# A second Strassen level for one more product, its operands in the large buffers, and another order of the steps

## The chip, the cores and the metric

The kernel runs on one core of a Trainium2 chip. Its engines are TensorE (PE; PEld is its weight load), VectorE (DVE), ScalarE (ACT), GpSimd (POOL) and SyncE (SP), whose queue issues nearly all transfers. The metric is device time in microseconds (us), as the median of several executions. A profile is one execution, recorded instruction by instruction.

## The reference

Eight sequences of 1024 tokens with 1024 features, all float32, get a cross attention and then a linear layer, each behind a layer norm and each added to its input:

```python
# x [8,1024,1024], memory m [8,64,1024], mask [8,64], factors [8,1024,1024], bias [1024]
x = x + attention(layernorm(x), m, mask)          # softmax(q m^T / 32) m, per sequence
x = x + einsum('btd,rde->bte', layernorm(x), factors) / sqrt(8) + bias
```

The sum over the eight factors does not depend on the token, so the kernel first adds the factors to one 1024 x 1024 matrix and then multiplies once.

## The kernel before, in words

**Groups and pairs.** The 8192 tokens are 16 groups `g` of 512: four row tiles `x[g, t]` of 128 tokens. Row tiles 0 and 2 are pair q = 0, tiles 1 and 3 pair q = 1 (`t = 2 h + q`).

**The attention of a group.** Tokens come twice: as row tiles (`load_rows`, L306) and as blocks (`load_blocks`, L295) which DVE transposes (`transpose_blocks`, L351). The first two groups are transposed by PE instead (`transpose_x_pe`, L377). `scores` (L394), `scores_back`, `softmax` (L422), `weights_back` and `read_out` (L460) are the attention; `residual` (L470, DVE) adds it to the rows. Row statistics come from DVE (`row_stats`, L336) or from ACT and POOL (`row_sums` and `row_squares`, L311 and L321).

**The second norm.** Per pair, either `norm_stats` (L480, DVE: two bn_stats of 512 columns and one aggregation for each h) or `norm_sums` and `norm_squares` (L499, L509: ACT passes and short POOL steps), then `normalize` (L525, ACT), which writes a large buffer `h`. `relayout` (L548) moves it by 16 transfers on SP's queue to `hb`, and `transpose_rows` (L557, DVE) makes `hT`. Group 0 is transposed by PE (`transpose_h_pe`).

**The big product.** Each pair has 256 rows, a 2 x 2 of blocks 128 rows x 512 features; the factor matrix is a 2 x 2 of 512 x 512 quadrants. A Strassen-Winograd scheme needs seven products instead of eight (`PRODUCTS`, L195). Row combinations s1 to s4 are `combine_rows` (L569, DVE), factor combinations t1 to t4 come out of `add_sums` (L711). `product g q p` (L587) is four matmuls of 128 x 512, each two records in the trace; `give` (L603, DVE) adds the result, scaled, from PSUM to one or two half row tiles.

**The second level.** For products 2, 3 and 4 (`SECOND`, L194) the two pairs together form a 2 x 2 again, with one operand of 256 rows, and seven smaller products take the place of two: `combine_parts` (L611, four DVE combinations of 128 x 256), `part` (L636, two matmuls of 128 x 256, four records) and `give_part` (L652, DVE, 256 columns for each of the product's outputs). The factor operands of the parts are four quadrants of the operand (one of them overwritten) and three new ones in `tau`, made once by `combine_factors` (L727).

**Factors.** The 32 `load_factor` transfers (1 MB each; s is the slice of rows, r the rank) are added up either on DVE (`add_factor`, L678) or on PE by an identity (`sum_factor`, L696, into PSUM).

**Buffers.** Large buffers of 8 KB a partition are handed out first in, first out (`Slots`, L155; `bigs`, L171): factors, `xb`, `xT`, `h`, `hb`, `hT` and the centred memory share eight. Row tiles have eleven slots, PSUM eight banks.

**Order.** Nothing reorders the work: `START` (L24) and `LOOP` (L78) are written-out lists of steps, and each engine and each DMA queue works off its own instructions in that order. `LOOP` runs 17 times; in it g is the group in its big product, p = g - 1, n = g + 1 (attention and norm), m = g + 2 (loads and scores). A step that is done already, or whose group doesn't exist, is skipped (`run`, L741).

```python
    SECOND = (2, 3, 4)
...
        5: ("s1", "t1", "v", True, ((1, 1), (0, 1)) if 3 in SECOND else ((1, 1),)),
...
    tau = const.tile([P, 3 * len(SECOND), 2 * HH], F32, name="tau")
```

Of the kernel before, what the change touches and what calls it, by code (L numbers as in the profile page):

```python
# [10 lines left out]
F32 = mybir.dt.float32  # L11
# [13 lines left out]
load_memory 0; load_factor 0 6; add_factor 0 6; centre_memory 0; load_rows 0 0; load_bias;  # L25
constants; load_factor 0 4; load_rows 0 3; load_rows 0 2; add_factor 0 4; load_rows 0 1;
load_factor 0 7; row_stats 0 0; transpose_x_pe 0 1; load_factor 1 2; row_stats 0 1;
transpose_memory 0; load_factor 0 0; transpose_x_pe 0 0; scores 0; masks; scores_back 0;
row_stats 0 2; add_factor 1 2; row_stats 0 3; add_factor 0 0; load_factor 0 5; load_factor 0 3;
load_factor 1 0; softmax 0; load_factor 1 5; sum_factor 0 5; load_factor 2 7; weights_back 0;  # L30
read_out 0 0 0; load_factor 0 2; add_factor 1 5; load_factor 2 6; add_factor 1 0; sum_factor 0 3;
read_out 0 0 1; residual 0 0 1; residual 0 0 0; load_factor 0 1; sum_factor 0 7; add_factor 0 2;
load_factor 2 4; read_out 0 1 1; norm_stats 0 0 0; sum_factor 0 1; load_rows 1 1; add_factor 2 6;
load_rows 1 0; norm_stats 0 0 1; add_factor 2 4; normalize 0 0 0; add_sums 0 1; residual 0 1 1;
normalize 0 0 1; load_factor 1 7; load_factor 2 3; load_factor 2 5; load_factor 1 4;
transpose_h_pe 0 0 0; sum_factor 2 7; add_factor 1 7; load_factor 1 3; transpose_x_pe 1 0;
load_factor 1 6; add_sums 0 0; transpose_h_pe 0 0 1; read_out 0 1 0; add_factor 2 3;
add_bias 0 0 2; add_bias 0 0 3; sum_factor 2 5; load_rows 1 3; load_factor 1 1; residual 0 1 0;
norm_stats 0 1 0; sum_factor 1 4; sum_factor 1 1; load_factor 2 1; load_rows 1 2;
combine_rows 0 0 1; sum_factor 2 1; norm_stats 0 1 1; add_factor 1 3; load_factor 2 2;  # L40
add_factor 1 6; load_factor 2 0; add_sums 1 1; row_sums 1 0; load_factor 3 0; add_sums 1 0;
transpose_x_pe 1 1; add_factor 2 2; add_factor 2 0; add_bias_v 0 0 0; add_bias_v 0 0 1;
add_sums 2 1; row_squares 1 0; load_factor 3 4; add_factor 3 4; scores 1; add_factor 3 0;
add_sums 2 0; product 0 0 1; load_factor 3 2; normalize 0 1 0; normalize 0 1 1;
transpose_h_pe 0 1 0; load_factor 3 3; add_factor 3 3; row_sums 1 1; load_factor 3 1;
load_factor 3 6; combine_rows 0 0 2; load_factor 3 7; transpose_h_pe 0 1 1; product 0 0 5;
row_squares 1 1; combine_rows 0 0 3; load_factor 3 5; add_factor 3 2; sum_factor 3 1;
combine_rows 0 0 4; scores_back 1; sum_factor 3 6; give 0 0 1; load_rows 2 1; load_rows 2 0;
add_factor 3 7; combine_rows 0 1 1; sum_factor 3 5; softmax 1; add_sums 3 1; row_sums 2 0;
product 0 1 1; weights_back 1; product 0 0 6; add_sums 3 0; read_out 1 0 0; combine_parts 0 4 1;  # L50
combine_factors 4; residual 1 0 0; read_out 1 0 1; combine_rows 0 1 2; part 0 4 2; give 0 0 6;
part 0 4 1; give_part 0 4 1; combine_parts 0 4 2; combine_rows 0 1 3; part 0 4 5; residual 1 0 1;
load_blocks 2 1; load_blocks 2 0; combine_rows 0 1 4; product 0 0 7; give 0 1 1;
norm_stats 1 0 0; row_squares 2 0; give_part 0 4 2; combine_parts 0 4 3; read_out 1 1 0;
add_bias 0 1 0; add_bias 0 1 1; norm_stats 1 0 1; product 0 1 6; part 0 4 6; combine_parts 0 2 1;
load_rows 2 2; residual 1 1 0; read_out 1 1 1; combine_parts 0 4 4; give_part 0 4 6; give 0 1 6;
residual 1 1 1; product 0 1 5; normalize 1 0 0; product 0 1 7; give_part 0 4 5;
combine_factors 3; normalize 1 0 1; load_memory 2; combine_factors 2; part 0 4 7; give 0 0 5;
give_part 0 4 7; give 0 0 7; part 0 4 3; part 0 2 1; transpose_blocks 2 0 0; part 0 2 5;
norm_sums 1 1; centre_memory 2; transpose_blocks 2 0 1; give_part 0 4 3; combine_parts 0 2 2;  # L60
give_part 0 2 1; transpose_blocks 2 0 2; part 0 4 4; combine_parts 0 3 1; transpose_memory 2;
relayout 1 0; give_part 0 4 4; part 0 3 1; part 0 3 2; add_bias 1 0 0; add_bias 1 0 1;
transpose_blocks 2 1 0; store 0 2; part 0 2 6; give_part 0 3 2; part 0 3 5;
transpose_blocks 2 1 1; give_part 0 2 5; norm_squares 1 1; transpose_blocks 2 0 3;
transpose_blocks 2 1 2; part 0 2 2; normalize 1 1 0; combine_parts 0 2 3; transpose_blocks 2 1 3;
normalize 1 1 1; give_part 0 2 6; combine_parts 0 2 4; combine_parts 0 3 2; transpose_rows 1 0 0;
scores 2; load_rows 2 3; transpose_rows 1 0 1; combine_rows 1 0 1; give_part 0 2 2; part 0 2 7;
# [40 lines left out]
def kernel(  # L108
# [632 lines left out]
    def run(line: str, groups):  # L741
        name, *args = line.split()
        args = [groups[a] if a in groups else int(a) for a in args]
        if groups:
# [3 lines left out]
            if name.endswith("memory") and g % GPB:  # L748
                return
# [38 lines left out]
```

## Time and profile before

| | us |
|---|---|
| median of 3 runs | 965.39 (964.19 to 966.02) |
| the profiled execution | 964.01 |
| its span | 962.2 |
| PE busy | 931.7 (97%) |
| DVE busy | 801.4 (83%) |
| ACT busy | 380.8 (40%) |
| POOL busy | 259.5 (27%) |
| transfers | 167.01 MB, mean 174 GB/s |

The span runs from the first to the last instruction on record; the remaining 1.8 us of the profiled execution lie around it. In a group's line of the profile the name left of the arrow is what is written, the names right of it what is read; `y4u` is a PSUM sum of parts of product 4, `yu` one of first-level products. Busy time is counted once where instructions of an engine overlap, while the mean is that of single records, so for pipelined work the distance between two starts tells more than a duration.

### The profile page before, as it was taken

The page shows a single profiled execution, that of the slowest core. Times are in us where ns is not written, and L with a number is a line of the kernel's source. Part 1 is how long each engine was busy: PE and PEld are TensorE (multiplying, and loading weights), DVE is VectorE, ACT ScalarE, POOL GpSimd, SP SyncE. Part 2 cuts the span into 40 slices and gives each one's busy share as a digit, 9 for nine tenths or more (in the row PEclk, how much of TensorE's full clock was granted, in tenths as well). Part 3 has the DMA queues.
Part 4 walks back from the last instruction along what each step waited for, and adds up shares of the span by engine and source line. Part 5 has one row for each costly group of instructions (what it writes and reads, how often), then busy time and mean ns, then how long its engine had stood idle before and what let it go on. Part 6 is the DMA issues. An engine that isn't in the chain of part 4 may idle for free.

```text
span 962.2 us, 11083 instructions
## 1 busy us (share of the span) xinstructions
PE 931.7 (97%) x3456; PEld 546.7 (57%) x3456; DVE 801.4 (83%) x1511; ACT 380.8 (40%) x712; POOL 259.5 (27%) x361
## 2 busy tenths in 40 slices
PE   3889999999999999999999999999999999999998
PEld 2345455655656565564656566564656566565656
DVE  3699999979799787988789787988789787988865
ACT  3036253443625254352724345351714445352300
POOL 0031125322322242421323142331324233232300
PEclk9999999999999999999999999999999999999999
DMA  9999736466565756457575746557575746552412
GB/s 352 419 421 397 182 101 145 127 184 156 160 163 161 162 171 153 135 159 174 157 167 159 169 140 158 141 170 175 154 180 153 174 112 181 139 158 79 101 66 87
DMA packets 93530, 167.01 MB, mean 174 GB/s; under 512 B 12320, under 2 KB 71840, under 8 KB 89376
## 3 DMA queue, kind: packets, MB, share of 16 engines
q1 hardware_dynamic: 93024, 165.20, 59.5%
q10 hardware_dynamic: 448, 1.11, 0.3%
q8 instruction: 27, 0.44, 0.2%
q14 instruction: 31, 0.25, 0.1%
HBM read 101.25 MB, written 33.55 MB: 140 GB/s over the span
## 4 chain that ended last, share of the span: by engine, by line
PE 87%; DMA 5%; DVE 5%; issue 1%; SPq 1%; ACT 0%; DVEq 0%; ACTq 0%
PE yu L594 33%; PE yv L594 11%; PE scT L401 6%; PE y3u L643 6%; PE y2u L643 6%; PE y4u L643 6%; PE ro L467 6%; DMA f<-in_L_ffn_factors_dram 4%; PE y4v L643 3%; PE y3v L643 3%; PE y2v L643 3%; PE y3z L643 1%; PE y2z L643 1%; PE y4z L643 1%; DMA x<-in_x_dram 1%; DVE b L691 1%
## 5 line engine op out<-in xcount | busy, mean ns | idle before, releaser
L543 POOL TENSOR_TENSOR x<-x,bias_bc 128x512 f32<-128x512 f32 x126 | 170.9, 1377 | 70.4 <-DVE x L607 35.8
L536 ACT ACTIVATE h<-x,nb,rstd 128x512 f32<-128x512 f32 x128 | 96.3, 825 | 211.4 <-DVE x L475 145.3
L594 PE MATMUL yu<-b,hT 128*128 128x512 f32 x256 | 118.0, 604 | 0.0
L594 PE MATMUL yu<-t,s 128*128 128x512 f32 x256 | 115.2, 593 | 0.0
L594 PE MATMUL yv<-t,s 128*128 128x512 f32 x256 | 115.2, 592 | 0.0
L594 PE MATMUL yu<-t,hT 128*128 128x512 f32 x256 | 115.1, 592 | 0.0
L607 DVE SCALAR_TENSOR_TENSOR x<-yu,x 128x512 f32<-128x512 f32 x128 | 83.2, 679 | 28.0 <-PE yu L594 28.0
L475 DVE SCALAR_TENSOR_TENSOR x<-ro,rden,x 128x512 f32<-128x512 f32 x128 | 88.5, 743 | 3.8 <-PE ro L467 3.8
L318 ACT ACTIVATE junk<-x 128x1024 bf16<-128x1024 f32 x60 | 63.3, 1055 | 49.1 <-DMA x<-in_x_dram 48.2
L594 PEld LDWEIGHTS yu<-b,hT 128*128 128x128 f32 x256 | 46.3, 189 | 62.6 <-issue 51.8
L358 DVE STREAM_TRANSPOSE xT<-xb 128x256 f32<-128x256 f32 x224 | 81.7, 411 | 0.0
L594 PEld LDWEIGHTS yu<-t,hT 128*128 128x128 f32 x256 | 48.6, 190 | 54.4 <-issue 50.2
L562 DVE STREAM_TRANSPOSE hT<-hb 128x1024 f32<-128x1024 f32 x60 | 73.6, 1228 | 3.1 <-DMA hb<-h 2.9
L594 PEld LDWEIGHTS yu<-t,s 128*128 128x128 f32 x256 | 48.5, 190 | 48.2 <-issue 45.7
L594 PEld LDWEIGHTS yv<-t,s 128*128 128x128 f32 x256 | 48.5, 190 | 48.2 <-issue 45.9
L492 POOL TENSOR_SCALAR rstd<-mv 128x2 f32<-128x2 f32 x17 | 4.6, 269 | 245.6 <-DVE mv L489 245.6
L330 ACT ACTIVATE junk<-x,nmean 128x1024 bf16<-128x1024 f32 x60 | 68.9, 1149 | 3.0 <-POOL nmean L319 0.8
L467 PE MATMUL ro<-mem,eT 64*128 64x512 f32 x256 | 64.5, 617 | 0.6 <-ACT eT L456 0.6
L657 DVE SCALAR_TENSOR_TENSOR x<-y3u,x 128x256 f32<-128x256 f32 x64 | 26.2, 410 | 44.6 <-PE y3u L643 44.4
L401 PE MATMUL scT<-xT,memT 128*64 128x256 f32 x512 | 60.5, 383 | 0.0
L504 ACT ACTIVATE junkz<-x 128x1024 bf16<-128x1024 f32 x30 | 31.7, 1056 | 67.7 <-DVE x L475 67.2
L706 PE MATMUL sum<-f,ident 128*128 128x512 f32 x96 | 43.7, 601 | 7.3 <-DMA f<-in_L_ffn_factors_dram 7.1
(133 smaller groups left out, 1495.5 us busy)
## 6 DMA issues: line engine op xcount, KB each, us to landing
f<-in_L_ffn_factors_dram SPq DMA_DIRECT2D x32, 1024.0 KB, 11.2
x<-in_x_dram SPq DMA_DIRECT2D x64, 512.0 KB, 4.5
out_dram<-x SPq DMA_DIRECT2D x64, 512.0 KB, 4.6
hb<-h SPq DMA_DIRECT2D x480, 64.0 KB, 2.0
xb<-in_x_dram SPq DMA_DIRECT2D x112, 256.0 KB, 7.0
mem<-in_ctx_dram SPq DMA_DIRECT2D x14, 256.0 KB, 3.9
mem<-in_ctx_dram ACTq DMA_DIRECT2D x2, 256.0 KB, 5.4
bias_bc<-in_L_ffn_bias_dram ACTq DMA_DIRECT2D x1, 512.0 KB, 7.8
```

The costliest lines, as they stand in the source:

```text
L318: nc.scalar.activation(junk, st["x", g, t], AF.Copy, accum_out=s1[:, t : t + 1])
L330: nc.scalar.activation(junk, st["x", g, t], AF.Square, bias=nmean[:, t : t + 1], accum_out=ss[:, t : t + 1])
L358: nc.vector.transpose(xT[:, 2 * e + c].rearrange("p (t j) -> p t j", j=Q), xb.rearrange("p t (k e i c) -> p e c t k i", e=NC // 2, i=2, c= ...
L401: nc.tensor.matmul(ps[ts(h, M), : 2 * P], mT[:, c, :], st["xT", g, h][:, c, :], start=(c == 0), stop=(c == NC - 1),)
L467: nc.tensor.matmul(ps, eT[ts(h, M), q, :], m[ts(h, M), ts(n, H)], start=True, stop=True)
L475: nc.vector.scalar_tensor_tensor(xt, st.pop(("ro", g, q, n, h)), rden[:, k : k + 1], xt, ALU.mult, ALU.add)
L536: nc.scalar.activation(to, fr, AF.Identity, bias=nb[:, h : h + 1], scale=rstd[:, h : h + 1])
L543: eng.tensor_add(xt, xt, bias_bc[:, ts(k % 2, H)])
L562: nc.vector.transpose(st["hT", g, q][:, h].rearrange("p c (t j) -> p t c j", j=Q), hb[:, h].rearrange("p t (c i) -> p t c i", i=Q),)
L594: nc.tensor.matmul(ps, lhs[:, c, :], wq[right][:, c, :], start=(first and c == 0), stop=(c == KH - 1), skip_group_check=True,)
L607: nc.vector.scalar_tensor_tensor(xt, st["y", g, q, key], ISR, xt, ALU.mult, ALU.add)
L643: nc.tensor.matmul(ps, lhs[:, c, :], wp[p][i][:, c, :], start=(first and c == 0), stop=(c == 1), skip_group_check=True,)
```

## The change

Product 5 is put among the second-level products. Its operand s1 of the two pairs is combined, and its factor operand t1 gets three more combinations. `tau` no longer has a place of its own: twelve operands, four to a buffer, lie in three large buffers that `combine_factors` takes and never gives back, and there are ten large buffers in place of eight. Parts 1, 2 and 3 read raw quadrants and may run ahead of `combine_factors`. Group 0 keeps the undivided product 5, and its steps of parts are skipped. The order is new throughout: `START` loads tokens of groups 0 and 1 ahead of the factors, and finishes more of group 1's attention early; slices s = 0, 1 and 3 of the factors come ahead of s = 2. Row statistics of group 1 move to `row_stats`, and the second norm of all groups goes by `norm_sums` and `norm_squares`; no bias addition is left on DVE.

```diff
 START = """
-load_memory 0; load_factor 0 6; add_factor 0 6; centre_memory 0; load_rows 0 0; load_bias;
-constants; load_factor 0 4; load_rows 0 3; load_rows 0 2; add_factor 0 4; load_rows 0 1;
...
+load_rows 1 0; constants; load_rows 0 0; load_rows 0 1; load_rows 0 2; load_memory 0;
+row_stats 1 0; load_rows 1 1; transpose_x_pe 0 0; row_stats 0 0; centre_memory 0; load_rows 0 3;
+transpose_x_pe 1 0; load_rows 1 2; masks; transpose_memory 0; load_factor 0 5; add_factor 0 5;
...
+sum_factor 2 7; load_factor 2 0; add_bias 0 0 3; add_factor 2 3; part 0 4 2; load_factor 2 5;
+combine_parts 0 4 2; add_factor 2 1; sum_factor 2 0; product 0 1 5; combine_rows 0 0 4;
+add_factor 2 4; give_part 0 4 2; combine_parts 0 4 3; load_memory 2; load_rows 2 0;
+normalize 1 0 1; relayout 1 0; add_factor 2 5; centre_memory 2; normalize 1 1 0; add_sums 2 1;
+product 0 0 6; load_blocks 2 1; add_sums 2 0; add_bias 0 1 3; give 0 0 6; transpose_memory 2;
+part 0 4 1; combine_factors 4; product 0 0 7; give_part 0 4 1; combine_parts 0 4 4; part 0 4 5;
...
+combine_rows 1 0 2; row_squares 2 0; combine_factors 3; relayout 1 1; scores 2; product 1 0 6;
+scores_back 2; give 0 1 7; combine_factors 5; give_part 0 2 6; part 0 3 6; part 0 2 2;
...
 LOOP = """
...
-add_bias g 1 3; combine_rows g 0 4; read_out n 1 0; norm_stats n 0 0; combine_rows g 1 2;
-read_out n 1 1; norm_stats n 0 1; transpose_blocks m 0 0; part g 4 5; end_rows p 1; end_rows p 0;
...
+load_blocks m 1; give_part p 3 7; part p 2 4; transpose_rows g 1 0; transpose_rows g 1 1;
+part p 3 4; weights_back n; combine_rows g 0 3; give_part p 3 2; give_part p 2 3; part p 3 3;
+combine_rows g 1 1; combine_rows g 0 4; load_blocks m 0; product g 1 1; give_part p 2 4;
+give_part p 3 4; give_part p 3 3; combine_parts g 5 1; read_out n 0 0; read_out n 0 1;
+part g 5 5; end_rows p 0; residual n 0 0; residual n 0 1; read_out n 1 0; residual n 1 0;
+norm_sums n 0; read_out n 1 1; combine_rows g 1 2; give g 1 1; give g 0 6; combine_parts g 5 2;
...
+transpose_rows n 0 0; normalize n 1 1; give_part g 5 4; give_part g 3 1; store g 2; scores m;
+combine_parts g 3 2; transpose_rows n 0 1; part g 3 5; product n 0 1; combine_rows n 0 1;
+combine_parts g 3 3; load_rows m 2; give_part g 2 6; give g 1 7; part g 3 6; row_sums m 1;
+scores_back m; relayout n 1; store g 3; combine_rows n 0 2; part g 2 7; add_bias g 0 1;
...
-    bigs = Slots(big, [f"big{i}" for i in range(8)])
+    bigs = Slots(big, [f"big{i}" for i in range(10)])
...
-    SECOND = (2, 3, 4)
+    SECOND = (2, 3, 4, 5)
...
-    tau = const.tile([P, 3 * len(SECOND), 2 * HH], F32, name="tau")
+    NTAU = 3 * len(SECOND)
+    tau = []
+    if NTAU % 4:
+        rest = const.tile([P, NTAU % 4, 2 * HH], F32, name="tau")
     wp = {}
-    for j, p in enumerate(SECOND):
+
+    def quadrant(p: int, i: int):
+
         w = wq[PRODUCTS[p][1]]
-        t1, t3, t4 = (tau[:, 3 * j + k, :].rearrange("p (c n) -> p c n", c=2) for k in range(3))
-        wp[p] = {1: w[:, :2, :HH], 5: t1, 6: w[:, :2, HH:], 3: w[:, 2:, HH:], 7: t3, 2: w[:, 2:, :HH], 4: t4}
+        return {1: w[:, :2, :HH], 3: w[:, 2:, HH:], 2: w[:, 2:, :HH]}[i]
...
+        right = quadrant(p, i) if i in (1, 2, 3) else wp[p][i]
...
-                wp[p][i][:, c, :],
+                right[:, c, :],
...
-        w = wp[p]
+        n = 3 * len(wp)
+        while len(tau) < n + 3:
+            k = len(tau)
+            four = rest if k >= NTAU - NTAU % 4 else bigs.take(("tau", k), [P, 4, 2 * HH], f"tau_{k}")
+            tau.extend(four[:, i, :].rearrange("p (c n) -> p c n", c=2) for i in range(four.shape[1]))
+        w = wp[p] = {i: quadrant(p, i) for i in (1, 2, 3)}
+        w.update({6: wq[PRODUCTS[p][1]][:, :2, HH:], 5: tau[n], 7: tau[n + 1], 4: tau[n + 2]})
...
+            if name in ("combine_parts", "part", "give_part") and ("product", g, 0, args[1]) in done:
+                return
```

## The prediction, made before the changed kernel was run

> **What bounds the kernel now.** I read the busy line first, then the slices, then the windows, the timeline of one period and the chain.
>
> ```profile
> PE 931.7 (97%) x3456; PEld 546.7 (57%) x3456; DVE 801.4 (83%) x1511; ACT 380.8 (40%) x712; POOL 259.5 (27%) x361
> ...
> PE   3889999999999999999999999999999999999998
> ...
> DVE  3699999979799787988789787988789787988865
> ...
> DMA  9999736466565756457575746557575746552412
> ```
>
> PE is full from the fourth slice to the last but one; DVE is close behind; the DMA engines are full for four slices, while the 32 factors stream in. So there are two regimes, and the windows give their sizes (columns: window, length, then busy time of PE, PEld, DVE, ACT, POOL, granted clock, DMA share, GB/s).
>
> ```profile
> 0.00:20.00 20.00, 3.71 (x17) 3.41 (x18) 6.26 (x11) 5.36 (x8) 0.96 (x8) 1.00 0.89 337
> 20.00:40.00 20.00, 18.94 (x90) 10.02 (x91) 12.18 (x18) 5.49 (x16) 1.23 (x2) 1.00 1.01 422
> 40.00:60.00 20.00, 15.34 (x60) 7.60 (x58) 18.35 (x24) 7.50 (x13) 3.86 (x6) 1.00 1.02 420
> 60.00:80.00 20.00, 17.40 (x62) 8.77 (x62) 17.75 (x23) 4.49 (x9) 4.41 (x5) 1.00 1.01 419
> 80.00:100.00 20.00, 19.10 (x74) 9.55 (x71) 19.90 (x23) 11.97 (x21) 3.67 (x5) 1.00 0.98 389
> ...
> 484.74:538.80 54.06, 54.06 (x201) 31.89 (x200) 45.42 (x88) 21.14 (x36) 14.79 (x22) 1.00 0.60 157
> ```
>
> Until 100 us PE works 74.5 us and idles 25.5: it waits for DMA. In a later period of 54.06 us (one loop pass, 484.74 to 538.80) it idles not at all, at full clock, and DVE works 45.4 us. After 100 us a microsecond off PE's work is a microsecond off the end, as long as nothing else comes late.
>
> **Part 1: product 5 by parts, PE.** Groups 1 to 15 lose two products (8 matmul records each) and gain seven parts (4 records each). Starts in the timeline give their real spacing; the durations overlap.
>
> ```profile
> 507.24 1.03 PE L643 MATMUL y4u<-t,r 128*128 128x256 f32 x4
> 508.10 3.60 PE L594 MATMUL yu<-t,s 128*128 128x512 f32 x8
> 511.53 1.03 PE L643 MATMUL y2v<-tau,r 128*128 128x256 f32 x4
> 512.40 1.03 PE L643 MATMUL y2u<-b,hT 128*128 128x256 f32 x4
> ```
>
> A product takes 511.53 - 508.10 = 3.43 us, a part 0.86 (nine parts run from 511.53 to 519.30: 0.863 each). 2 x 3.43 - 7 x 0.863 = 0.82 us less per group, **12.3 us** in 15 groups. The new parts have the form of the 336 measured ones, so a part that costs more is excluded.
>
> **Part 1: DVE.** Starts again:
>
> ```profile
> 479.78 0.42 DVE L657 SCALAR_TENSOR_TENSOR x<-y3u,x 128x256 f32<-128x256 f32 x1 [3.20 <-PE y3u L643]
> 480.12 0.68 DVE L607 SCALAR_TENSOR_TENSOR x<-yu,x 128x512 f32<-128x512 f32 x1
> 480.71 0.42 DVE L657 SCALAR_TENSOR_TENSOR x<-y2u,x 128x256 f32<-128x256 f32 x1
> ```
>
> A give of 512 columns costs 0.59, one of 256 costs 0.34. Product 5 feeds two outputs, so each part is given twice: 14 x 0.34 = 4.8 against 4 x 0.59 = 2.4. The four combinations of the new product cost (35.0 + 34.2 + 24.1 + 19.9) / 48 = 2.4 us by their groups. The new loop takes the statistics of both halves of the normalization on ACT, which removes two norm_stats (2 x (2 x 0.64 + 0.21) = 3.0 us). Sum: +1.8 us, DVE 47.2 of 53.2 us (89%, now 84%). ACT gains 2 x (1.06 + 0.19 + 1.15 + 0.19) = 5.2, about 29 of 53. Neither reaches PE; that slack is what hides these edits, and a DVE instruction that PE waits for costs its delay if the slack is used up.
>
> **Where a rule speaks against it.** The row:
>
> ```profile
> L629 DVE TENSOR_TENSOR hT<-hT,hT 128x256 f32<-128x256 f32 x48 | 35.0, 730 | 0.0
> ```
>
> The median of these is 418 ns, the longest 1491 ns, and the long ones (1.36 and 1.49 us at 512.60 and 513.88) lie under POOL's bias additions (512.40 to 515.08). The Trainium skill (SBUF — State Buffer, Who interferes with whom) says that a DVE instruction with two SBUF inputs is shut out while a GpSimd instruction reads SBUF, and one with a single SBUF input is not. By that only the four combinations per group can be held, not the 14 gives, which read PSUM; were each held for a whole bias addition of 1377 ns (the row of L543), DVE would stand at 47.2 + 5.5 = 52.7 us of 53.2, with no slack left. By the rows the means already hold such waits (2.4 us, not 4 x 0.34), and I take those.
>
> **Part 2: three of ten large buffers.** After the start seven serve the loop instead of eight. I followed each take to the release it reuses. Most have 5 to 18 us of PE work between. The thin one: in every other group h of the second pair takes the buffer that relayout of the first pair frees. Relayout is 16 DMAs on SP's queue:
>
> ```profile
> 504.99 10.18 SPq L553 DMA_DIRECT2D hb<-h  x16
> ```
>
> plus 2.0 us to land. The chain in a new pass, counted from its start: last residual of the second pair at 19, ACT's two row sums (2.5) and the first pair's normalize (3.0) to 24.5, relayout 12.2 to 36.7, second normalize 3.0 to 39.7, second relayout 12.2 to 51.9. Its transpose is wanted at the next pass's start plus 2.8 us less 1.2, 54.8: slack 2.9 us. So I charge nothing; queued behind a late second relayout on SP are only store g 3 and the next blocks, and its waiter is DVE, then PE. Store g 2 stands ahead of it on SP and needs its tile's last give: rival 2 has the price. The Trainium skill (Perfetto Trace Analysis, Optimization Strategy) warns that the same gap repeated on the busy engine can mean too few buffers for the next tile; before shows no such gap, and the rule has no price.
>
> **Part 3: tokens first.** Before, PE's first transpose starts at 16.29 us, behind two factors and four row tiles. The new order asks for rows ahead of all factors: two row tiles behind one other, 2.1 MB with the memory, against 4.7 MB before. At the first window's 337 GB/s those 4.7 MB are 14.0 us, 2.3 short of 16.29; so 6.2 + 2.3 = 8.5 us. That is worth only what is done before the next barrier. The chain shows it:
>
> ```profile
> 93.19 6.06 DMA f<-in_L_ffn_factors_dram
> 99.29 3.71 PE sum L706 x8
> ```
>
> The last factor lands at 99.2, and product 6 of group 0 needs t2, so all factors; it starts at 106.48. Both orders issue the same 38.8 MB up to the last factor (32 of 1.05 MB, eight row tiles, memory, bias), so it can't land much earlier than 99; ten buffers instead of eight let the loads run as far ahead. Then, new: add_factor 2.3 us, two sums 1.2, t2 1.15 gives 103.8; DVE may be behind, so I take 105, **1.5 us** earlier. Bounds: 420 GB/s throughout lands it at 95.5, product 6 at 100 (-6.5); a stalled SP queue, +4. What PE has done by then: all that it had before plus the four read_outs of group 1 (4 x 0.96), product 0 1 5 (3.43) and one part (0.86): **8.1 us** more. In all that is 42.8 for sums, 13.7 for products, 0.9, 13.6 for transposes, 15.7 for scores, weights and read-outs: 87 us of the 96 from 8.5 on. DVE worked 80.4 us of the first 106.2 before, from 12.75 on; with four more residuals (5.3) and its other new work at most 88, of the 100 from 5 on. Twelve sum_factor and 20 add_factor stay as they were, and norm_stats of group 0 and row statistics of group 1 change places between DVE and ACT: nothing.
>
> After that barrier DVE is the late one. From product 6 on, `scores 2` follows five products, eleven parts and the memory's transposes, 17.2 + 9.5 + 0.6 = 27.3 us of PE. It reads the blocks that DVE transposes, and ahead of the last of them DVE has add_sums 2.3, two combine_factors 5.2, four gives 3.0, nine part gives 3.0, twelve combinations 6.1, two transpose_rows 2.3 and eight transpose_blocks 5.5: 27.4 us by free spacings. From 106.5 to 165.2 DVE took 57.9 us for work that I count at 54.1 in the same way, 7% over: 29.3, after 1.2 for t3, 30.5. That is 3 us of waiting; with a second, smaller one where parts of product 3 need combine_factors 3, **4 us** back. Bounds 0 and 8 (twice that).
>
> **Tail.** The last pass has the same end, a few parts, then stores; one bias addition (1.38 us) is put at the end, but on POOL, which is idle, for a half tile whose last give isn't the last. Nothing, at most 1.4.
>
> **Sum.** Span 962.2 - 12.3 - 1.5 - 8.1 + 4 = 944.3; the profiled execution took 964.0 for that span, 1.8 us outside it, so **946** us. The runs' median, 965.39, is 0.14% above the profiled time, inside the 0.2% that a measurement of this kernel can tell from no change.
>
> **Rivals.**
> 1. *Waits eat part of it* (20%). DVE at 89% has no spare in the passages where it leads PE by under 1 us (combine_parts 5 1 is listed directly ahead of part 5 5, behind one product). If PE waits 0.8 us in each of 15 groups, the Strassen saving is gone and the start's remains: 958. For it: the "DVE x <- PE y" waits show that DVE runs just behind PE; against it: PE idled 0.0 us in the period above.
> 2. *Slower* (14%): the second relayout comes late behind store g 2. SP's waits at L668 for DVE's combinations are 86.3 us in 22 and 56.8 in 9, 4.6 us each. One such wait against a slack of 2.9 in 14 groups costs 24 us: 970. It makes the kernel slower than before when the 18 us of gain are used up, that is from 1.3 us of PE idle per group, a wait of 4.2 us. Against it: the tile of store g 2 gets its last give some 4 us of PE work before the store's place.
> 3. *The start goes better* (8%): DMA full throughout, no wait at `scores 2`: 946 - 5 - 4 = 937.
> That the change doesn't do what it says has no room in the steady groups; in group 0 product 5 stays undivided, which the count of 15 holds.
>
> **How the numbers follow.** Forecast 946 (58%, own range 940 to 952). The range reaches down to rival 3's 937 and up through most of rival 1, 962; out of it are rival 2 and a little. Faster by over 0.2% (under 963.5): 0.83; within: 0.03; slower: 0.14.
>
> **What would show it.** PE busy near 919 us; no L594 matmul of yv after the start (t1's product), 28 parts per group; steady period 53.2; DVE near 89%; first transpose at 8 to 9 us; product 6 of group 0 at 105; a wait of PE at scores 2. I would be wrong if PE shows the same idle in every pass (on DVE: rival 1; on hb: rival 2), or if the first 100 us still hold 25 us of idle.

## The result, and the profile after

The changed kernel takes **949.24 us** (median of 4 runs, 948.81 to 951.26) against 964.79 us for the kernel before on the same chip (964.02 to 966.02): ratio 0.9835, 95% interval 0.9823 to 0.9847. It was predicted at 946.0, range 937 to 962. The profiled execution took 949.06 us, its span is 947.2 us, so 1.9 us lie outside the span.

The page of the changed kernel, busy line and three of its slices:

```profile
PE 921.2 (97%) x3636; PEld 579.9 (61%) x3636; DVE 794.2 (84%) x1633; ACT 453.2 (48%) x832; POOL 278.3 (29%) x359
...
PE   4979999999999999999999999999999999999998
...
PEclk9979999999999999999999999999999999999999
DMA  9979876567484856658484756648484755641412
```

PE's work fell from 931.7 to 921.2 us, near the 919 that was predicted, and from the fourth slice on PE is as full as before. But the third slice has a dent in three rows at once: PE, the granted clock and DMA. In the profiled execution of before the clock was at full speed throughout and DMA stood at 9 for four slices. (The profile of before shows one execution with a mean granted clock of 1.00; 27 of its 34 executions timed beside the later runs had 0.995 or 0.996, and all four of the changed kernel 0.993 or 0.994.) The sum came out nearly right while one of its terms was badly wrong, and it is hidden there.

**The loop** does what was forecast. From the start of one group's `scores` to that of another twelve groups on, the chain of before gives (853.27 - 197.72) / 12 = 54.63 us a group:

```profile
197.72 3.60 PE scT L401 x32
...
853.27 3.60 PE scT L401 x32
```

and that of the changed kernel (837.49 - 192.88) / 12 = 53.72:

```profile
192.88 3.60 PE scT L404 x32
...
837.49 3.60 PE scT L404 x32
```

That is 0.91 less, against 0.82 predicted; in 600 us from 250 on PE idles 0.15 us.

**The start** does not. Product 6 of group 0, which needs all factors, begins at 114.43 us, where before had 106.48 and the prediction 105. The timeline of PE in before:

```profile
106.48 3.60 PE L594 MATMUL yu<-t,s 128*128 128x512 f32 x8
```

and in the changed kernel:

```profile
114.43 3.70 PE L597 MATMUL yu<-t,s 128*128 128x512 f32 x8 [1.11 <-DVE t L726]
```

From there to the end it takes 947.2 - 114.4 = 832.8 us, against 962.2 - 106.5 = 855.7 before. To see why that product is late, read the windows of the changed kernel around the dent (window, length, busy PE, PEld, DVE, ACT, POOL, granted clock, DMA share, GB/s):

```profile
44.00:48.00 4.00, 3.17 (x12) 1.08 (x11) 4.00 (x5) 0.00 (x0) 4.00 (x1) 1.00 1.02 426
...
52.00:56.00 4.00, 1.31 (x8) 0.88 (x8) 1.90 (x2) 3.97 (x7) 0.00 (x0) 0.86 1.02 426
56.00:60.00 4.00, 2.56 (x4) 0.99 (x4) 0.66 (x1) 3.97 (x8) 0.22 (x1) 0.50 1.00 418
60.00:64.00 4.00, 3.86 (x6) 1.68 (x7) 3.48 (x6) 0.07 (x1) 1.10 (x3) 0.50 0.65 270
64.00:68.00 4.00, 4.00 (x13) 1.93 (x12) 1.03 (x2) 0.00 (x0) 0.00 (x0) 0.86 0.02 6
```

In time order: POOL is busy for 4 us with one instruction while DVE is full; then PE starves; then the clock falls to half; then DMA stops, in the middle of loading the factors. The timeline of the changed kernel has the first link:

```profile
43.42 1.22 DVE L695 TENSOR_TENSOR b<-b,f 128x1024 f32<-128x1024 f32 x1
43.58 6.78 POOL L522 TENSOR_SCALAR rstd<-zq 128x2 f32<-128x2 f32 x1 [2.63 <-ACT junky L518]
...
49.09 1.23 DVE L695 TENSOR_TENSOR t<-t,f 128x1024 f32<-128x1024 f32 x1
50.22 1.41 DVE L478 SCALAR_TENSOR_TENSOR x<-ro,rden,x 128x512 f32<-128x512 f32 x2
...
51.47 3.02 ACT L539 ACTIVATE h<-x,nb,rstd 128x512 f32<-128x512 f32 x4 [7.97 <-POOL nb L525]
...
57.23 2.56 PE L470 MATMUL ro<-mem,eT 64*128 64x512 f32 x4 [3.15 <-ACT hT L377]
```

A step on two numbers per partition, 0.19 us at 60.16, takes 6.78 us. It begins just after the first of six additions of factors on DVE, each with two inputs in SBUF, and ends at 50.36, 0.14 us after DVE has come to `residual`, which reads PSUM. ACT waits 7.97 us for it, PE waits for ACT, and PE's later matmuls run at half clock (four read-outs in 2.56 us, elsewhere 1.1). The loads stop at 62 us because no large buffer comes back: SP's queue waited up to 15.9 us in one place for PE's transposes, whose input `h` would have freed one.

### The profile page after: what moved, and what is told of

Read it like the earlier page. It is cut to its first block, busy times and chain, and to the rows that moved or that the text cites. A ratio compares the mean times of both kernels' runs of the same rounds, so it can differ in the third digit from the quotient of the medians.

```text
span 947.2 us, 11708 instructions
## 1 busy us (share of the span) xinstructions
PE 921.2 (97%) x3636; PEld 579.9 (61%) x3636; DVE 794.2 (84%) x1633; ACT 453.2 (48%) x832; POOL 278.3 (29%) x359
## 4 chain that ended last, share of the span: by engine, by line
PE 90%; DVE 5%; DMA 1%; issue 1%; POOL 1%; ACT 1%; SPq 0%; DVEq 0%; ACTq 0%
PE yu L597 34%; PE ro L470 6%; PE scT L404 6%; PE y5u L647 6%; PE y2u L647 6%; PE y4u L647 6%; PE y3u L647 6%; PE y3v L647 3%; PE y5v L647 3%; PE y2v L647 3%; PE y4v L647 3%; DVE b L695 2%; PE y2z L647 1%; PE y3z L647 1%; PE y5z L647 1%; PE y4z L647 1%
## 5 line engine op out<-in xcount | busy, mean ns | idle before, releaser
L507 ACT ACTIVATE junkz<-x 128x1024 bf16<-128x1024 f32 x64 | 67.6, 1057 | 109.3 <-DVE x L478 108.3
L597 PE MATMUL yu<-b,hT 128*128 128x512 f32 x256 | 115.1, 593 | 0.1
L597 PE MATMUL yu<-t,hT 128*128 128x512 f32 x256 | 112.6, 592 | 0.0
L478 DVE SCALAR_TENSOR_TENSOR x<-ro,rden,x 128x512 f32<-128x512 f32 x128 | 88.6, 745 | 17.8 <-PE ro L470 17.7
L509 POOL TENSOR_SCALAR zm<-zs 128x2 f32<-128x2 f32 x32 | 13.2, 411 | 248.6 <-ACT junkz L507 248.6
L518 ACT ACTIVATE junky<-x,zm 128x1024 bf16<-128x1024 f32 x64 | 73.5, 1149 | 13.6 <-POOL zm L509 11.3
L597 PEld LDWEIGHTS yu<-b,hT 128*128 128x128 f32 x256 | 48.5, 190 | 49.2 <-issue 47.2
L321 ACT ACTIVATE junk<-x 128x1024 bf16<-128x1024 f32 x56 | 59.0, 1054 | 30.4 <-DMA x<-in_x_dram 29.8
L333 ACT ACTIVATE junk<-x,nmean 128x1024 bf16<-128x1024 f32 x56 | 64.3, 1149 | 7.5 <-POOL nmean L322 5.3
L404 PEld LDWEIGHTS scT<-xT,memT 128*64 128x64 f32 x512 | 35.3, 137 | 21.1 <-issue 4.3
L322 POOL TENSOR_SCALAR nmean<-sum 128x2 f32<-128x2 f32 x28 | 7.5, 267 | 136.1 <-ACT junk L321 136.1
## 6 DMA issues: line engine op xcount, KB each, us to landing
x<-in_x_dram SPq DMA_DIRECT2D x64, 512.0 KB, 3.6
out_dram<-x SPq DMA_DIRECT2D x64, 512.0 KB, 3.2
mem<-in_ctx_dram ACTq DMA_DIRECT2D x2, 256.0 KB, 10.2
bias_bc<-in_L_ffn_bias_dram ACTq DMA_DIRECT2D x1, 512.0 KB, 8.1
```

The source lines that it names most:

```text
L404: nc.tensor.matmul(ps[ts(h, M), : 2 * P], mT[:, c, :], st["xT", g, h][:, c, :], start=(c == 0), stop=(c == NC - 1),)
L478: nc.vector.scalar_tensor_tensor(xt, st.pop(("ro", g, q, n, h)), rden[:, k : k + 1], xt, ALU.mult, ALU.add)
L507: nc.scalar.activation(junk, st["x", g, 2 * h + q], AF.Copy, accum_out=s1[:, h : h + 1])
L518: nc.scalar.activation(junk, st["x", g, 2 * h + q], AF.Square, bias=nmean[:, h : h + 1], accum_out=ss[:, h : h + 1])
L597: nc.tensor.matmul(ps, lhs[:, c, :], wq[right][:, c, :], start=(first and c == 0), stop=(c == KH - 1), skip_group_check=True,)
```

## Experiments

**Theory S** (starved step): POOL's step is the root, and clock, buffers and the hole in DMA follow from it. **Rival O**: the order on ACT, which has two more passes (54.39 to 56.6) ahead of the copy of hT, is the root. **Rival M**: the last factor is late through the large buffers alone, so that none of the first three moves changes the time (949). The first four kernels were timed beside before at 965.70 us, the next four beside 965.40, three more beside 964.70, the last beside 964.04.

### 1. Two residuals between the additions

```diff
-residual 0 1 1; load_factor 1 7; residual 0 1 0; add_factor 0 6; add_factor 1 7; sum_factor 1 0;
+load_factor 1 7; add_factor 0 6; residual 0 1 0; add_factor 1 7; residual 0 1 1; sum_factor 1 0;
```

> START alone is changed: the two residuals of group 0's second pair move from ahead of three add_factor steps into the run of them (one behind add_factor 0 6, one behind add_factor 1 7). They read PSUM, so the run of DVE additions with two SBUF inputs is broken at 45.7 and 49.3 us. Theory S (a 0.2 us POOL step of group 0's norm was shut out for 6.8 us by that run; the late h idles PE, PE's clock falls, buffers come back late, DMA idles 6 us, product 6 of group 0 starts at 114.4 in place of 105): the POOL step rstd takes under 1 us, h of the first pair starts near 47 in place of 51.5, granted clock 1.00 from 50 to 70, no hole in the DMA rate at 62 to 68, product 6 at 106 to 108, time 941 to 944. Rival O (the order on ACT is the root: the row sums of the second pair stand ahead of the copies of hT): PE still waits 2 to 3 us for hT, clock still falls, time 947 to 949. Rival M (the last factor is late by the slots alone): no change, 949.

945.29 us, ratio 0.9787 (0.9765 to 0.9809); product 6 at 110.29. POOL's step took 0.92 us and ended as `residual` began:

```profile
46.30 0.92 POOL L519 TENSOR_SCALAR rstd<-zq 128x2 f32<-128x2 f32 x1 [2.63 <-ACT junky L515]
```

An earlier step of POOL, 0.32 us in the changed kernel, now stood under two additions; it took 2.59 us and ended at 43.67, 0.17 us after the residual behind them began. DMA still fell, but to 0.54 at 62 to 66, and the clock to half for 3.4 us, behind a wait of PE of 1.69 us for the moved residual. The direction is S's and M falls; the full clock, the full DMA and product 6 at 106 to 108 did not come, and the time is 1.3 us over S's range.

### 2. ACT's order

```diff
-normalize 0 0 1; norm_sums 0 1; sum_factor 1 4;
+normalize 0 0 1; sum_factor 1 4;
...
-transpose_h_pe 0 0 0; read_out 1 0 0;
+transpose_h_pe 0 0 0; norm_sums 0 1; read_out 1 0 0;
```

> START alone is changed: norm_sums 0 1 (two ACT passes, 2.3 us) moves from ahead of transpose_h_pe 0 0 0 to behind it. Theory S: h still comes at 51.5, PE still idles from 50 to 54, only the 2.3 us of ACT passes leave the wait for hT; PE resumes at 54.5 in place of 57.2; whether the clock falls decides between 944 (it does not) and 947 (it does). Rival O: the whole delay goes, product 6 at 106 to 108, 941 to 944. Rival M: 949.

947.69 us, ratio 0.9818 (0.9797 to 0.984); product 6 at 113.34, POOL's step still 6.78 us, clock 0.50. O is not the root: product 6 comes 1.1 us earlier, and the interval of the ratio overlaps that of the changed kernel. S's 947 for a clock that falls was 0.7 too low.

### 3. PE's transposes later

```diff
-transpose_h_pe 0 0 0; read_out 1 0 0;
+read_out 1 0 0;
...
-transpose_h_pe 0 0 1; load_factor 0 0;
+transpose_h_pe 0 0 0; transpose_h_pe 0 0 1; load_factor 0 0;
```

> START alone is changed: transpose_h_pe 0 0 0 moves behind two read_outs and a sum_factor (5.5 us of PE work) to just ahead of transpose_h_pe 0 0 1. The late h is left as it is. Theory S and its consequences (PE idle, then clock, then buffers, then DMA): PE has work while h is late, so the clock stays at 1.00, no DMA hole, product 6 at 106 to 109, 942 to 945, although the POOL step is still shut out for some 6 us. If the lost time is in the late h itself and not in the idle PE: under 2 us better, 947 to 949. Rival M: 949.

945.82 us, ratio 0.9795 (0.9771 to 0.982); product 6 at 111.51. POOL's step is as long as ever (6.78 us), but PE has other work in the meantime, and the time is 3.4 us shorter; M falls here too. S's expectation was missed all the same: PE now waits 1.81 us for a residual, the clock is at 0.50 from 55 to 62, DMA falls to 0.42 at 62 to 64, and product 6 and the time lie outside 106 to 109 and 942 to 945. So the loss can be made smaller at either end of the chain, but in the profiles neither move takes it away.

### 4. The new order without the cut

Product 5 undivided in all groups, everything else of the change kept; three of ten large buffers still go to the operands, with three of their twelve places unused.

```diff
-    SECOND = (2, 3, 4, 5)
+    SECOND = (2, 3, 4)
...
-part g 5 5; part g 5 6;
+product g 0 5; product g 1 5;
```

> The changed kernel with product 5 undivided in all groups: its seven parts, their combinations and gives are left out of the loop, product g 0 5 stands where part g 5 5 stood and product g 1 5 where part g 5 6 stood, with gives behind; combine_factors 5 is left out; order, buffers and start otherwise the same. Theory (the part cut is worth its PE time, 0.91 us per group by the two loop periods): 949.2 + 13.7 = 963, period 54.6 us. By the 0.82 us of the prediction: 961.5. Rival (the loop's gain is from the order or from fewer switches between sizes): well under 960. If the new start is worth nothing, this kernel stands level with the one before (964.8); if its delay of product 6 outweighs the 8.1 us done early, slower.

966.92 us, ratio 1.0025 (1.0007 to 1.0043): level with before or a little above. The expected 963 was missed by 4 us; in the profiled execution of this kernel product 6 comes at 117.61, 3.2 us later than in the changed kernel, and the clock is at half for 13.7 us ahead of it instead of 10.2. The cut is worth 966.9 - 949.2 = 17.7 us in this order (18.3 by the ratios). The period by the chain is (856.67 - 198.82) / 12 = 54.82, so 1.10 a group or 16.5 us of that come from the loop; the new order alone makes the period 0.19 longer than before's. DVE's share in 600 us of loop is 74.7% (41.0 us a group) here, 84.8% (45.6) with the cut: the cut adds 4.6 us of DVE work a group, where the prediction's pieces (4.8 - 2.4 + 2.4) say 4.8.

### 5. Six pauses in DVE's run

The sharpest test of S: nothing is moved, and DVE gets more work.

```diff
             nc.vector.tensor_add(w, before[:, :, ts(n, H)] if before is not None else w, f[:, :, ts(n, H)])
+            if (s, r) in ((0, 6), (1, 7), (1, 2)):
+                gap = small.tile([P, 2], F32, tag="gap", name=f"gap_{s}_{r}_{n}")
+                nc.vector.reciprocal(gap, neghalf[:, :2])
```

> The changed kernel with six short DVE instructions more: a RECIPROCAL of 128x2 into a tile that nobody reads, one behind each addition of add_factor 0 6, 1 7 and 1 2; no order is changed. It parts two readings of the 6.78 us that POOL's 128x2 step took. A: POOL is shut out by the run of two-input additions as such, and any pause in the run lets it in: the step then ends within 1.5 us, its two followers get in at the next pauses, ACT's normalization starts at 46 to 48.5 instead of 51.47 us, product 6 of group 0 starts at 109 to 112, time 944 to 947. B: it needs an instruction that reads PSUM, as the residual, or the step is slow for another reason: still 6.8 us, product 6 at 114 to 115, 949 to 950.

**943.35 us**, ratio 0.9771 (0.9752 to 0.979). Six instructions more on a busy engine make the kernel 5.9 us faster. The timeline of this kernel, its POOL and DVE lines:

```profile
43.62 1.11 POOL L522 TENSOR_SCALAR rstd<-zq 128x2 f32<-128x2 f32 x1 [2.63 <-ACT junky L518]
44.59 0.16 DVE L698 RECIPROCAL gap<-neghalf 128x2 f32<-128x2 f32 x1
44.67 1.20 DVE L695 TENSOR_TENSOR t<-t,f 128x1024 f32<-128x1024 f32 x1
44.81 1.64 POOL L523 TENSOR_TENSOR rstd<-rstd,neghalf 128x2 f32<-128x2 f32 x1
45.79 0.16 DVE L698 RECIPROCAL gap<-neghalf 128x2 f32<-128x2 f32 x1
...
46.52 0.60 POOL L525 TENSOR_TENSOR nb<-zm,rstd 128x2 f32<-128x2 f32 x1
46.98 0.16 DVE L698 RECIPROCAL gap<-neghalf 128x2 f32<-128x2 f32 x1
```

Each of POOL's three steps gets through at a pause: the first ends at 44.73 (pause at 44.59), the third at 47.12 (pause at 46.98); the second, which takes 0.71 us where nothing is in its way, ends at 46.45, 0.66 after the pause at 45.79. And the windows of this kernel, same columns as above:

```profile
56.00:60.00 4.00, 4.00 (x11) 1.58 (x9) 2.95 (x5) 0.93 (x2) 1.10 (x3) 1.00 1.02 424
60.00:64.00 4.00, 3.76 (x16) 2.04 (x14) 3.50 (x5) 3.06 (x5) 0.00 (x0) 1.00 1.01 410
64.00:68.00 4.00, 4.00 (x10) 1.71 (x9) 4.00 (x5) 4.00 (x7) 0.53 (x1) 1.00 1.01 408
```

The clock is full, DMA is full, and product 6 starts at 108.27. Reading A holds, with a time 0.7 us under its range and product 6 0.7 us ahead of it; reading B falls, and S is shown as the root of the dent. The rest of the lateness, 108.27 against 105, is another matter: the last factor now lands at 95.00 + 8.11 = 103.1 us instead of the assumed 99. The first 20 us move 289 GB/s here and 337 before, which is 0.96 MB or 2.3 us at 420 GB/s: with the new order the DMA engines are as busy at the very start (0.90 against 0.89) but move less. Why, and where the other 1.8 of the 4.1 us go, I have not traced.

### 6 and 7. The cures together

Run 6 has the edits of runs 1 and 3, run 7 those of 1, 2 and 3.

> The changed kernel with both moves that helped alone: residual 0 1 0 and 0 1 1 stand between the additions (945.29 alone), and PE's first transposes of h of group 0 stand directly ahead of the second ones (945.82 alone). If each takes away a different wait in the same stretch (theory S: POOL's step, then PE's place in the order), PE's idle time between 46 and 62 us falls under 4 us, the granted clock stays over 0.9, the DMA engines have no hole at 62 to 66, product 6 starts at 106 to 109 and the time is 941 to 943.5. If both take away the same wait, 945.

948.21 us, ratio 0.9818 (0.9788 to 0.9849). Missed: together they are no better than each alone. The four executions lie between 944.24 and 950.38, and the interval overlaps those of runs 1 and 3, so that worse is not shown. The profile is that of the longest one; PE's timeline in it:

```profile
48.74 2.54 PE L467 MATMUL ro<-mem,eT 64*128 64x512 f32 x4 [2.33 <-DVE x L475]
51.21 6.29 PE L707 MATMUL sum<-f,ident 128*128 128x512 f32 x8
```

PE waits 2.33 us for the residual that stands between the additions (1.69 in run 1), the clock is at 0.50 from 52 to 56, and eight sums take 6.29 us instead of 3.7. SP then waits for PE's sums (10.4 us) and transposes (8.9), DMA falls to 0.47 at 64 to 68, and product 6 starts at 114.39. So the loss has a second entrance: in the profiles of runs 1, 3, 6 and 7 a wait of PE in this stretch, a halved clock and a fall of DMA at 62 to 68 us follow one another, in 1, 6 and 7 without POOL's long step. How much of it goes with the clock, the executions show: in each of these four kernels one had a mean granted clock of 1.00, and took 943.17 (run 1), 943.58 (run 3), 944.24 (run 6) and 943.69 us (run 7). All others of the same four programs had 0.994 to 0.998 and took 944.34 to 950.38. Without a fall of the clock the four kernels lie within 1.1 us of one another.

> As the kernel before this one, and norm_sums 0 1 also behind transpose_h_pe 0 0 0, so that ACT copies hT first. Alone this was worth 1.5 us (947.69 against 949.24). By S, in which ACT's order is only a small part: 0 to 1.5 us under the kernel with both moves, 940 to 943. With the transposes moved down behind it, norm_sums 0 1 may come too late for the second pair's norm; then it is slower than that kernel by 1 to 2 us.

945.18 us, ratio 0.9791 (0.9775 to 0.9808), product 6 at 110.86; the wait of 2.33 us and a fall of the clock are there too, but shorter. Missed by 2 us.

### 8. The old order with the cut

Before's order; the parts of product 5 put around the place of the second product by hand, and the operands in three of ten buffers. Two transposes of rows and two of blocks change places, or eight buffers would be needed at once.

```diff
-product g 1 1; combine_parts g 4 1; product g 0 7;
+product g 1 1; combine_parts g 5 2; part g 5 5; combine_parts g 4 1; product g 0 7;
...
-transpose_rows n 0 0; give g 1 7;
+transpose_blocks m 1 2; give g 1 7;
```

> The order of before, with product 5 of groups 1 to 15 by parts and three of ten buffers for the factor operands: the two products and their gives taken out of the loop, the parts, their combinations and their gives put in around the place of the second product by hand, combine_factors 5 put behind combine_factors 2 at the start; two transpose_rows and two transpose_blocks change places, so that seven buffers suffice. If the cut is worth what it takes off PE wherever it stands: 965.7 less 12 to 14, 952 to 955 with a start like that of before (product 6 of group 0 at 106 to 107), and 28 parts a group at 0.863. If it pays only in the order that came with it (DVE too late for the parts, or buffers): PE idles in every pass, and it is 960 or more.

1117.92 us, ratio 1.1573 (1.1549 to 1.1597): far beyond the first expectation, and much worse than the second one's 960. Two things stand in the waits above all: PE's part y5z behind residuals (28.9 us, my placement), and SP's relayout (137.3 us in 7 waits, up to 20.9) for the buffer of the centred memory, which PE has yet to transpose; row loads stand behind it on SP.

### 9. Seven buffers in the old order, nothing cut

```diff
-    bigs = Slots(big, [f"big{i}" for i in range(10)])
+    bigs = Slots(big, [f"big{i}" for i in range(9)])
...
-    SECOND = (2, 3, 4, 5)
+    SECOND = (2, 3, 4)
```

(with before's START and LOOP, and the same four steps exchanged)

> The kernel before with one thing of the change alone: the factor operands lie in two of nine large buffers, so that seven serve the loop; nothing of product 5 is cut. Two transpose_rows and two transpose_blocks change places in the loop, as in the kernel that took 1118 us, since eight would be in use at once without that. If the buffers are what made that kernel slow (its relayout waited 137.3 us in 7 cases, up to 20.9, for the transposed memory to leave the buffer that it reuses, and row loads stood behind it on SP): the same wait in every second group here, 14 to 20 us each, 1060 to 1120 us. If it was the hand-placed parts (y5z behind the residuals 28.9 us, gives of y5u): 965 to 985.

1020.52 us, ratio 1.0571 (1.0547 to 1.0596): between the two expectations. SP's waits in this kernel, total, times and longest:

```profile
SPq L553 <- PE memTp L288: 93.0, 7, 13.6
```

The same 7 waits. So the seven buffers, with the exchange that they need, cost 55.8 us in the old order, and the hand-placed parts, less what the cut saves, some 97 us more. In the changed kernel no relayout waits for PE's transposes of the memory. The two runs don't price the cut itself (run 4 does); they show that "three buffers for operands" is free only in an order made for it.

### 10. Pauses, and ACT's order

The edits of runs 5 and 2.

> The changed kernel with the six short DVE instructions (943.35 alone) and with norm_sums 0 1 behind transpose_h_pe 0 0 0 (947.69 alone, 1.5 us of gain). With POOL's step let in, PE still idled some 1.6 us at 48 to 56 us, part of it on ACT. If that part is still ACT's order: 0.5 to 1.5 us less, 942 to 943, product 6 no earlier than 107.5, since the last factor now comes over a DMA that is full from 40 to 102 us. If the DMA alone sets it: 943.4.

**942.29 us** (941.30 to 945.14), ratio 0.9771 (0.9749 to 0.9793), product 6 at 108.09. With run 5 the fastest of the study, ahead of both kernels; the difference between those two is within their scatter. In their profiles run 10 keeps the full clock after product 6, while run 5 loses 1.7 us there: `scores 2` comes 27.7 and 29.4 us behind it.

### 11 and 12. How much slack DVE has

```diff
+            if p == 5:
+                more = small.tile([P, 6], F32, tag="more", name=f"more_{g}_{i}_{h}")
+                nc.vector.bn_stats(more, xt)
```

> The changed kernel with more work on DVE in the loop and nothing else: behind each of the 14 gives of parts of product 5 a bn_stats of the same 128x256 into a tile that nobody reads, some 0.35 to 0.4 us each, 5 to 5.6 us a group in 15 groups, DVE at 94 to 95% of a period instead of 85%. If DVE's slack hides such work as the prediction has it (PE has no DVE wait in the loop): within 2 us of the changed kernel, 948 to 951. If DVE runs so close ahead of PE that each give's delay reaches PE (rival 1's price, 0.8 us a group or more): 960 or more, with PE waiting for DVE at y5u.

1017.77 us, ratio 1.0543 (1.0521 to 1.0566): DVE's slack does not hide such work, and the loss is far over the 960 of the other reading. Each `bn_stats` took 0.43 us, 6.0 a group; 68.5 us came out at the end, 4.6 a group. PE's waits for DVE in this kernel, the three largest:

```profile
PE y4u L647 <- DVE r L630: 23.3, 13, 1.8
PE y4u L647 <- DVE x L661: 9.9, 26, 0.6
PE y2u L647 <- DVE r L630: 9.4, 13, 0.9
```

PE waits for combinations and gives that come late, of other products than the one that got the extra work, and not at y5u as expected: the delay travels along DVE's queue. Run 12 has half of it (`if p == 5 and h == 0`).

> The changed kernel with half the added DVE work: a bn_stats of 128x256 (0.43 us measured) behind 7 of the 14 gives of parts of product 5, those with h = 0; 3.0 us a group in 15 groups. The full amount, 6.0 us a group, cost 68 us, 4.6 a group, so that 1.4 us a group were hidden. T: DVE has one stretch per period with little to spare, and what goes over that is paid in full: 3.0 less 1.4 is 1.6 us a group, 24 us, 973 (968 to 978). L: each give that comes late is paid in proportion: half of 68, 983 (980 to 987). W: the slack is wider than 1.4 and the full dose met something else on the way (row loads behind stores, say): 949 to 960.

988.31 us, ratio 1.0253 (1.0233 to 1.0273): none of the three, L being the nearest. 39 us for 3.0 us a group in 15 groups is 2.6 a group, so only some 0.4 us a group were hidden at this place; the second half of the dose cost less than the first (2.0 a group). PE's listed waits for DVE sum to about 20 us here, and PE's busy time grew by 16.6 us at the same clock; that part I have not traced further. Windows of the changed kernel, each a ninth of a period, show where the slack is not:

```profile
466.97:472.94 5.97, 5.97 (x23) 3.91 (x23) 2.88 (x7) 3.97 (x8) 2.38 (x4) 1.00 0.47 104
472.94:478.91 5.97, 5.97 (x23) 3.73 (x22) 3.32 (x7) 1.44 (x8) 0.00 (x0) 1.00 0.66 169
...
484.88:490.84 5.96, 5.96 (x27) 3.76 (x26) 5.71 (x10) 3.60 (x7) 0.49 (x1) 1.00 1.11 233
490.84:496.81 5.97, 5.97 (x21) 3.77 (x20) 5.94 (x11) 5.29 (x9) 4.54 (x6) 1.00 0.46 166
496.81:502.78 5.97, 5.97 (x15) 2.68 (x15) 5.94 (x19) 5.79 (x10) 2.87 (x4) 1.00 0.49 177
502.78:508.75 5.97, 5.97 (x27) 4.81 (x26) 5.94 (x17) 3.87 (x6) 4.19 (x7) 1.00 0.40 88
```

DVE's 45.99 us of 53.72 are not spread: from 484.9 to 508.8 it works 23.5 of 23.9 us, and it rests above all from 467 to 479, where it works 6.2 of 11.9 us. Six of the seven pairs of gives of product 5 stand between 490.8 and 512.0.

## Why the prediction was right, and where it was not

| step | predicted | measured |
|---|---|---|
| 15 groups with the cut | -12.3 | -13.7 (15 x 0.91, cut and order together) |
| product 6 of group 0 | -1.5 | +7.95 (114.43 against 106.48) |
| PE's work done ahead of it | -8.1 | -9.2 (-22.9 from product 6 to the end, less the loop's -13.7) |
| wait at scores 2 | +4 | 0 |
| span | -17.9 | -15.0 |

- **The cut** was right, and run 4 shows that it is the cause: without it the new order is level with before. In before the products that went away took 3.43 us each, as priced. In run 4, over two periods of PE's starts, the four cost 14.1 us where they stood, 3.53 each, since one followed by another shape (read-outs) takes up to 3.63; so the cut is worth 1.10 a group in the new order, which by itself costs 0.19; 0.91 is left. The steady period came to 53.7 and not 53.2 because the pass of 54.06 us that it was counted from is the shorter of two that alternate (538.80 to 594.00, the next one, is 55.20; the mean is 54.63).
- **The start** is the step that failed, and one sentence of it: that norm_stats of group 0 and the row statistics of group 1 "change places between DVE and ACT: nothing". By `norm_stats` POOL's short steps stood behind DVE's own statistics and took 0.23, 0.71, 0.19 and 0.22 us in before (47.25 to 48.86), the first of them:

```profile
47.25 0.23 POOL L492 TENSOR_SCALAR rstd<-mv 128x2 f32<-128x2 f32 x1 [22.62 <-DVE mv L489]
```

By `norm_squares` they come from ACT at any moment, and came in the middle of six additions: 6.78 us for the first of them, and product 6 6.2 us later than in run 5, where the pauses let it in. The upper bound of that term (+4) was too small as well; the forecast of -1.5 was 9.5 us off. The rule of the Trainium skill (SBUF — State Buffer, Who interferes with whom) that I had weighed against the combinations of the loop holds in this case in the other direction too: POOL was the one shut out. What the same section states, that the order of issue decides who waits, does not give the changed kernel's lines by itself: the step began at 43.58, ahead of five of the six additions, and ended only behind the last. By those lines and run 5's, DVE keeps POOL out from one such addition to the next as long as no other instruction stands between.
- **Work done ahead** came out as counted, as far as a remainder can show it: 9.2 is what is left over, 8.1 were counted, and 0.9 is a wait at 135 us that before had.
- **No wait at scores 2.** In the changed kernel PE comes to it 27.7 us after product 6 and does not wait:

```profile
142.02 0.76 DVE L361 STREAM_TRANSPOSE xT<-xb 128x256 f32<-128x256 f32 x2
...
142.13 3.67 PE L404 MATMUL scT<-xT,memT 128*64 128x256 f32 x32
```

DVE ends its last transposes at 142.78, 28.3 us after product 6 began, where 30.5 were counted; and PE, which starts at 142.13, does not need them for its first matmuls. So the sum of DVE's work was 2.2 us too high, and the rest of the 3 us is that PE does not wait for the last block. That the late barrier merely gave DVE time is made unlikely by run 10: product 6 stands 6.3 us earlier there, `scores 2` again 27.7 us behind it (135.79), without a wait.
- **DVE at 89%** was wrong: 45.6 us a group (84.8%), below before's 46.4. The cut's +4.6 and the removed norm_stats' -3.0 (28.2 + 4.6 us in 11 groups) were as priced. What I left out: the two-input instructions of DVE fell from 160.1 to 129.9 us in 11 groups from before to run 4, 2.7 a group, as fewer of them met POOL's bias additions in the new order: by the traces, 71 overlap one in before and take 31.7 us more than the shortest of their kind, 43 in run 4, 6.6 us more (39 and 21.2 us in the changed kernel). ACT's "about 29" was right (28.7), though the row shown gives 21.1 + 5.2 = 26.3; that pass is a light one, the mean of before is 23.9.
- **"That slack is what hides these edits"** was right only in its result. The steady windows show no wait of PE, but runs 11 and 12 show that about 0.4 us a group was left behind the gives of product 5, not the 6 that 89% suggests. Rival 1 was much closer than its 20% and its argument; by the share of the busy line that cannot be seen.
- **Rival 2** did not happen, though its ground was thin: in the changed kernel DVE waits for a relayout in 21 cases, mostly and longest for the second one of a group, against 3 before (2.9 us); yet PE never waits for DVE in the steady loop.

```profile
DVE hT L565 <- DMA hb<-h: 47.7, 21, 4.0
```

- **Other signs.** PE's first transpose starts at 9.06 us (8 to 9 forecast), and the first 100 us hold 20.3 us of idle PE, less than the 25 that would have spoken against the prediction.

## What to carry to other kernels

When a change moves short POOL steps from behind DVE's own work to behind another engine's, look up what DVE does at the time they now arrive: a run of two-input SBUF instructions held one of them here until the run ended, and a cheap instruction between was the cure. Read an engine's slack from the stretch in which it is full, not from its share of the span, and test it with a measured dose of extra work before counting on it. Check a prediction term by term even when its sum is right: here a total within 0.4% hid a term that was 9.5 us off, offset for the most part by three others.

## What the runs showed of the hardware

- A POOL instruction of 0.2 us took 6.78 us during six back-to-back additions of 1.23 us on DVE; here and in runs 1 and 5 steps of 0.2 to 0.3 us that were held so ended 0.14 to 0.17 us after the start of a DVE instruction without two SBUF inputs. In the other direction DVE lost 2.9 us a group to POOL's bias additions in before (31.7 us in 11 groups).
- The granted clock fell to 0.50 around waits of PE of 3.15 us (changed kernel, with shorter ones ahead), 2.33 (run 6) and 1.69 (run 1), but not after 3.6 us without a matmul in before (42.5 to 46.1). In run 5 a wait of 2.14 us ahead of product 6 was followed by 3.4 us at 0.50; in run 10, 1.71 us in the same place did nothing. So the length of the gap alone does not decide.
- What the clock records of these traces show: in the dent the stretches at 0.50 lasted 3.4 us (runs 1, 7), 6.8 (runs 3, 6), 10.2 (changed kernel, run 2) and 13.7 (run 4), and the stretch at full speed ahead of the changed kernel's fall 37.55 us, all of them multiples of 3.41 us. So the clock changes at points 3.41 us apart, and it counts where a wait lies between them. In the 3.41 us ahead of the fall PE was busy for 1.31 us in the changed kernel, 1.83 in run 1, 1.08 in run 6 and 1.30 in run 5 (ahead of 109.57). The gap in before lies across such a point, with 1.71 and 1.50 us of work on its two sides, and the clock stayed; so it did with 1.70 in run 10. Little work in such a stretch goes with a fall, but 1.83 against 1.50 shows that busy time does not decide alone. The Trainium skill (TensorE: Matmul & The Clock Gate, Part 1) speaks of a free-running window of some 3.4 us, after an idle one of which the clock falls: the spacing agrees, the idle window does not, since PE worked in all of these stretches.
- In the changed kernel the stall of PE and its halved clock kept buffers from coming free, and the DMA engines stood still for 4 us (0.02 at 64 to 68) in the most transfer-bound part of the kernel. No run changes the clock alone; the executions named at run 6 are the nearest to it.
